# The head of a four-layer convolution kernel: GpSimd's table powers queued behind the first image's norm, TensorE's diagonals built ahead of the tables

## Chip, cores and metric

The kernel runs on one core of one Trainium2 chip. The metric is the device time of one launch in microseconds (us). Differences are told against the kernel before, and times of single events are given from the start of the profiled span.

## What is computed

The input is 32 images of 96 channels, 56 x 56. Four layers follow each other, each of the form x = x + f(norm(x)), where the norm takes groups of three channels of an image. Layer 0 is an inverted bottleneck with a gate, layer 1 a wavelet convolution, layer 2 a quantised bottleneck, layer 3 a 9 x 9 convolution with one diffusion kernel for each channel. Only the parts that the change touches are shown:

```python
# the norm ahead of each layer
g = v.reshape(B_, G, C_ // G, H_, W_)
m = jnp.mean(g, axis=(2, 3, 4), keepdims=True)
s = jnp.var(g, axis=(2, 3, 4), keepdims=True)
return ((g - m) / jnp.sqrt(s + eps)).reshape(v.shape)
...
# layer 0
h = jnp.einsum('nchw,oc->nohw', x, w_exp)
h = jax.nn.silu(_bn(h, g1, b1, m1, v1))
h = jax.lax.conv_general_dilated(h, w_dw, window_strides=(1, 1), padding='SAME', feature_group_count=MID, ...)
h = jax.nn.silu(_bn(h, g2, b2, m2, v2))
s = h.mean(axis=(2, 3))
s = jax.nn.silu(s @ w_se1.T + b_se1)
s = jax.nn.sigmoid(s @ w_se2.T + b_se2)
h = h * s[:, :, None, None]
h = jnp.einsum('nchw,oc->nohw', h, w_proj)
h = _bn(h, g3, b3, m3, v3)
return h + identity
...
# layer 3: the diffusion kernels, 9 x 9 for each channel
gauss = 1.0 / (4.0 * math.pi * tg) * jnp.exp(-r2 / (4.0 * tg))
poi = math.gamma(1.5) / math.pi ** 1.5 * tp / jnp.power(tp * tp + r2, 1.5)
return val * gauss + (1.0 - val) * poi
```

The exponential of `gauss` and the power of `poi` are both computed as elementwise powers on GpSimd.

## The kernel before

**Layer 0, image by image.** The 576 middle channels are five blocks of 128 (the last one half full). For each image ScalarE sums the pixels and their squared deviations (L287, steps `s` and `q`), TensorE adds them over the channel groups (L292, `u` and `v`), VectorE makes mean and variance (L302, L306), GpSimd raises the variance to the power -1/2 (`deviation`, L308, the tile `rstd`), VectorE makes the bias from it (`norm_bias`, L312, the tile `nb`), and ScalarE normalises (L321, the tile `xn`). TensorE expands the channels (L335), ScalarE applies silu and writes into padded tiles (L347). The depthwise 3 x 3 convolution is shared out: for blocks 0 to 2 ScalarE makes the first tap (L355, step `f`) and VectorE the other eight (L360, step `t`), one instruction of 128 x 3136 elements each; for blocks 3 and 4 TensorE multiplies with diagonal matrices (L388, steps `a` and `c`), which are built once from the weights (L262, the tile `diag`). Then come silu (L366), the gate (L412 to L436), the projection on TensorE (L447 to L449), the residual sum on VectorE (L455), and the statistics for the next norm (L87).

**The order.** `L0_ORDER` is a list of steps written out by hand. A `+` or `-` behind a step means the next or the previous image. `run_steps` goes through it once for each image, from two ahead of the first to two after the last. Under `manual_schedule` the order of PE, VectorE and ScalarE for these steps is that of the list; GpSimd and SP, and all that stands outside, are ordered by the scheduler.

**The tables.** Layers 1 and 3 need banded matrices. Their rows are made by `tables()`, called in `layer0` ahead of the steps. It opens a pool of its own (`tables`) and calls three functions. `diffusion_kernels` makes the 9 x 9 kernels: VectorE r2 (L1134 to L1141), then GpSimd two powers of 96 x 81 elements (L1145, L1146) and the sum (L1147 to L1149). `wavelet_filters` fills three tables on VectorE (L510 to L549), zeroes its rooms on GpSimd (L538, the third on VectorE), and sends each out by a DMA on SP (L550, tensor `zwav`); the third table is built in the room of the first. `diffusion_filters` copies the kernels on GpSimd (L1158, the tile `rev`), zeroes the room of the second table (L1160), fills it with 16 copies (L1167), and sends it out (L1168, tensor `zdiff`). Many small DMAs on SP then spread the rows into matrices in HBM (L559, L586).

**The late pool.** When `tables()` returns, its pool is closed, and a pool `late` (`l0l`) is opened in its room. It holds three of the five tap buffers `h2s` (numbers 2 to 4), `hab` and `hc` (outputs of TensorE's depthwise part), `wg` (gated projection weights) and the second pair of images. Whoever writes a tile of it first waits for the tables' last DMA. Two such writers stand in the head: `eye2`, a slice of `wg` (L259), from which the 18 diagonals are multiplied (L262), and the DMA that fetches images 2 and 3 (`fetch(2)`, L211).

Of the kernel before, what the change touches and what calls it, by code (L numbers as in the profile page):

```python
# [10 lines left out]
F32 = mybir.dt.float32  # L11
# [4 lines left out]
ALU = mybir.AluOpType  # L16
# [4 lines left out]
B, C, H, W = 32, 96, 56, 56  # L21
# [5 lines left out]
NT = RT * W  # L27
W2 = W // 2
NPH = 4
W4 = W // NPH  # L30
HH = H // 2
PH = HH * NPH
NP = H // (2 * RT)
# [16 lines left out]
K_GAUSS = VAL / (4.0 * math.pi * TG)  # L50
K_POI = (1.0 - VAL) * math.gamma(1.5) / math.pi**1.5 * TP
# [7 lines left out]
MANUAL = {mybir.EngineType.PE, mybir.EngineType.DVE, mybir.EngineType.Activation}  # L59
MANUAL_SP = MANUAL | {mybir.EngineType.SP}  # L60
L0_ORDER = """
# [10 lines left out]
L2_ON_DVE = {"e00", "e20", "a301", "a201"}  # L72


class Shared:


# [35 lines left out]
    tc.keep_in_program_order(nc.sync.dma_start(dram, row))  # L113


def run_steps(step, image, order):


    for n in range(-2, B + 2):
        for s in order.split():  # L120
            b = n + s.count("+") - s.count("-")
            if 0 <= b < B:
                step[s[0]](image(b), *map(int, s.rstrip("+-")[1:]))


# [51 lines left out]
def layer0(ctx, tc, S, x, w, y0, norm1, tables, aside):  # L177
# [10 lines left out]
    nc = tc.nc  # L188
    cp = ctx.enter_context(tc.tile_pool(name="l0c", bufs=1))
# [5 lines left out]
    ND = NBLK + 1  # L195
    COL = (0, 1, 2, 3, 5)
    HALF = 64
# [7 lines left out]
    pairs = [cp.tile([C, H * NPH, 2, W4], F32, tag="xt0", name="xt0")]  # L205

    def fetch(b):

        if b < B:
            pair = pairs[b // 2 % 2]  # L210
            nc.sync.dma_start(pair, x[b // 2])  # L211
            for j in range(2):
                xs[b + j] = pair, pair[:, :, j, :]
# [13 lines left out]
    for j in range(2):  # L227
        g, b_, m, v = (mid[:, 4 * j + i, :] for i in range(4))
# [3 lines left out]
        s = cp.tile([128, ND], F32, tag=f"s{j}", name=f"s{j}")  # L232
# [16 lines left out]
    mv_all = cp.tile([C, B, 2], F32, tag="mv0", name="mv0")  # L249
    h2s = [cp.tile([128, H, W], F32, tag=f"h2{i}", name=f"h2{i}") for i in range(2)]  # L250


    tables()
    late = ctx.enter_context(tc.tile_pool(name="l0l", bufs=1))
    h2s += [late.tile([128, H, W], F32, tag=f"h2{i}", name=f"h2{i}") for i in (2, 3)]
    hab = late.tile([128, NP, 2, NT], F32, tag="hab", name="hab")
    wg = late.tile([128, ND + 1, C], F32, tag="wg", name="wg")
    eye2 = wg[:, 0, :HALF]
    nc.vector.tensor_tensor(eye2, S.ident[:, :HALF], S.ident[:, HALF:], ALU.add)  # L259
    for k in (AB, CC):  # L260
        for t in range(9):
            nc.vector.tensor_scalar(diag[:, k - AB, t, :], eye2, wdw[:, COL[k], t : t + 1], None, ALU.mult)  # L262
    h2s.append(late.tile([128, H, W], F32, tag="h24", name="h24"))
    hc = late.tile([128, 2, 2, NT], F32, tag="hc", name="hc")
    pairs.append(late.tile([C, H * NPH, 2, W4], F32, tag="xt1", name="xt1"))
    fetch(2)

    ims = {}

# [12 lines left out]
    def sums(im, name, func, bias):  # L282

        im[name] = sm.tile([C, NP], F32, tag=name, name=name)
        for i in range(NP):
            junk = pool.tile([C, 2 * RT * NPH, W4], BF16, tag="junk", name="junk", bufs=1)
            nc.scalar.activation(junk, im["xt"][:, i * 2 * RT * NPH : (i + 1) * 2 * RT * NPH], func, bias=bias,  # L287
                                 accum_out=im[name][:, i : i + 1])

    def group_sum(im, name):  # L290
        ps = psm.tile([C, NP], F32, tag="sm", name="pn")
        nc.tensor.matmul(ps, S.grp, im[name], start=True, stop=True)  # L292
        im["ps" + name] = ps

    def total(im, name):
        t = sm.tile([C, 1], F32, tag=f"t{name}", name=f"t{name}")
        nc.vector.tensor_reduce(t, im["ps" + name], AX.X, ALU.add)
        return t
# [5 lines left out]
    def deviation(im):  # L304
        ve = sm.tile([C, 1], F32, tag="ve", name="ve")
        nc.vector.tensor_scalar(ve, total(im, "s2"), 1.0 / HW, EPS_GN, ALU.mult, ALU.add)  # L306
        im["rstd"] = sm.tile([C, 1], F32, tag="rstd", name="rstd")
        nc.gpsimd.tensor_tensor(im["rstd"], ve, S.mhalf[:C, :1], ALU.pow)  # L308

    def norm_bias(im):  # L310
        im["nb"] = sm.tile([C, 1], F32, tag="nb", name="nb")
# [148 lines left out]
    def store(im):  # L460
# [11 lines left out]
    step = {  # L472
        "s": lambda im: sums(im, "s1", AF.Identity, 0.0), "u": lambda im: group_sum(im, "s1"), "m": mean,
        "q": lambda im: sums(im, "s2", AF.Square, im["nm"]), "v": lambda im: group_sum(im, "s2"),
        "w": deviation, "b": norm_bias, "n": normalise, "r": residual,
        "e": expand, "f": first_tap, "t": tap, "z": end_block, "a": depthwise_ab, "c": depthwise_c,
        "g": lambda im, i: (totals, squeeze, excite, gates, gated)[i](im),
        "p": project, "d": add, "o": store,
    }
    with tc.manual_schedule(engines=MANUAL):  # L480
        run_steps(step, image, L0_ORDER)
    store_norm(tc, S, sm, psum, mv_all, norm1, S.bias1)


# [637 lines left out]
    store_norm(tc, S, sm, psum, mv_all, norm3, None)  # L1122


def diffusion_kernels(nc, cp, w):

    n = KS * KS
    dm = cp.tile([C, 4], F32, tag="dm", name="dm")
    nc.sync.dma_start(dm, w["l3_dm"])
    yy = cp.tile([C, 2, n], F32, tag="yy", name="yy")  # L1130
    nc.sync.dma_start(yy, w["grid"])
    z = cp.tile([C, 2, n], F32, tag="z", name="z")
    for i in range(2):
        nc.vector.tensor_scalar(z[:, i, :], yy[:, 0, :], dm[:, 2 * i : 2 * i + 1], None, ALU.mult)  # L1134
        nc.vector.scalar_tensor_tensor(z[:, i, :], yy[:, 1, :], dm[:, 2 * i + 1 : 2 * i + 2], z[:, i, :],
                                       ALU.mult, ALU.add)
    nc.vector.tensor_tensor(z, z, z, ALU.mult)
    r2, arg, kern = z[:, 0], z[:, 1], yy[:, 0]
    nc.vector.tensor_tensor(r2, z[:, 0], z[:, 1], ALU.add)
    nc.vector.tensor_scalar(arg, r2, K_EXP2, None, ALU.mult)  # L1140
    nc.vector.tensor_scalar(r2, r2, TP * TP, None, ALU.add)  # L1141

    nc.gpsimd.memset(yy[:, 0], 2.0)
    nc.gpsimd.memset(yy[:, 1], -1.5)
    nc.gpsimd.tensor_tensor(kern, yy[:, 0], arg, ALU.pow)  # L1145
    nc.gpsimd.tensor_tensor(r2, r2, yy[:, 1], ALU.pow)  # L1146
    nc.gpsimd.tensor_scalar(kern, kern, K_GAUSS, None, ALU.mult)  # L1147
    nc.gpsimd.tensor_scalar(r2, r2, K_POI, None, ALU.mult)
    nc.gpsimd.tensor_tensor(kern, r2, kern, ALU.add)  # L1149
    return kern  # L1150


# [82 lines left out]
def kernel_body(tc, w, x, out):  # L1235
    nc = tc.nc
    with ExitStack() as ctx:
        cp = ctx.enter_context(tc.tile_pool(name="shared", bufs=1))
        dp = ctx.enter_context(tc.tile_pool(name="scratch", bufs=1, space=DRAM))
        S = Shared()  # L1240
        S.ident = cp.tile([128, 128], F32, tag="ident", name="ident")
        S.grp = cp.tile([C, C], F32, tag="grp", name="grp")
        S.mhalf = cp.tile([128, B], F32, tag="mhalf", name="mhalf")
        nc.gpsimd.memset(S.mhalf, -0.5)
        S.bias1 = cp.tile([C, 1], F32, tag="bb", name="bb")

        def scratch(name, shape):
            return dp.tile(shape, F32, tag=name, name=name)

        y0, y1, y2 = ([scratch(f"y{i}_{g}", [GR, H * NPH, B, W4]) for g in range(C // GR)] for i in range(3))
        norm1, norm3 = (scratch(f"norm{i}", [C, 2 * B + 1]) for i in (1, 3))
        z1, z2 = (scratch(f"zwav{v}", [C, 2, NPH, LEN * NK * NPH]) for v in (1, 2))
        z3 = scratch("zwav3", [C, 2, 2, LEN * KW * 2])
        zd = scratch("zdiff", [C, 1, NPH, LEN * NK * NPH])

        t1, td = (scratch(f"t{n}", [C, (HH + 2 * HALO) * NPH, NK * PH]) for n in ("wav1", "diff"))
        t2 = scratch("twav2", [C, PH, NK * PH])
        t3 = scratch("twav3", [C, HH, KW * HH])  # L1260

        def tables():
            with tc.tile_pool(name="tables", bufs=1) as tp:
                kernels = diffusion_kernels(nc, tp, w)
                room = wavelet_filters(nc, tp, w, z1, z2, z3)
                diffusion_filters(nc, tp, kernels, zd, room)

        layer0(tc, S, x, w, y0, norm1, tables,
               [lambda c=c: wavelet_matrices(nc, z1, z2, z3, t1, t2, t3, c) for c in range(C)]
               + [lambda c=c: matrix_rows(nc, td[c], zd[c], 1) for c in range(C)])  # L1270
        with ExitStack() as ctx2:
            k2 = Layer2(ctx2, tc, S, w, y1)

            def behind(pair):
                k2.prepare(pair)
                if not k2.stages:
                    k2.begin(min(2 * pair, C - GR))

            layer1(tc, w, y0, norm1, t1, t2, t3, y1, behind)
            k2.begin(C)  # L1280
            layer2(tc, S, k2, y1, y2, norm3)
        layer3(tc, w, y2, norm3, td, out)
# [121 lines left out]
```

## Time and profile before

| what | us |
|---|---|
| median of 3 runs | 6427.65 |
| lowest and highest of them | 6418.2, 6427.76 |
| the profiled execution | 6420.77 |
| its span | 6419.0 |
| PE busy, of the span | 6013.8 |
| VectorE busy | 5173.8 |
| ScalarE busy | 4052.9 |
| GpSimd busy | 223.1 |

In the profile, PE is TensorE's matmuls, PEld its weight loads, DVE is VectorE, ACT is ScalarE, POOL is GpSimd, SP is the engine that issues the DMAs. L12 is line 12 of the kernel before. A row of the timeline has start, duration, engine, line, operation, output and input tiles (buffer numbers left out), shape and count; the bracket at its end tells how long the engine was idle before it and what ended that. A row of waits names the engine and tile that waited, who released it, and then the total in us, how often, and the longest. The granted clock is that of TensorE as a share of full speed. The mean granted clock over the whole span was 0.975.

### The profile page before, as it was taken

The page shows a single profiled execution, that of the slowest core. Times are in us where ns is not written, and L with a number is a line of the kernel's source. Part 1 is how long each engine was busy: PE and PEld are TensorE (multiplying, and loading weights), DVE is VectorE, ACT ScalarE, POOL GpSimd, SP SyncE. Part 2 cuts the span into 40 slices and gives each one's busy share as a digit, 9 for nine tenths or more (in the row PEclk, how much of TensorE's full clock was granted, in tenths as well). Part 3 has the DMA queues.
Part 4 walks back from the last instruction along what each step waited for, and adds up shares of the span by engine and source line. Part 5 has one row for each costly group of instructions (what it writes and reads, how often), then busy time and mean ns, then how long its engine had stood idle before and what let it go on. Part 6 is the DMA issues. An engine that isn't in the chain of part 4 may idle for free.

```text
span 6419.0 us, 115759 instructions
## 1 busy us (share of the span) xinstructions
PE 6013.8 (94%) x49064; PEld 3571.1 (56%) x49064; DVE 5173.8 (81%) x5533; ACT 4052.9 (63%) x5716; POOL 223.1 (3%) x157
## 2 busy tenths in 40 slices
PE   4999999999999999999969999989999999999699
PEld 2444444444444444444435666668777777777344
DVE  6999999999999999999947666667676766776587
ACT  4676666766766667667535566567676766766355
POOL 4000000000000000000000000000000000000000
PEclk8999999999999999999979999999999999999899
DMA  3022221222211222113365866558787686964988
GB/s 95 6 48 53 45 46 32 49 55 47 42 32 43 54 49 42 32 37 40 23 86 142 150 148 146 130 30 54 39 53 41 51 43 44 51 42 29 174 254 245
DMA packets 1305765, 452.95 MB, mean 71 GB/s; under 512 B 1123151, under 2 KB 1301063, under 8 KB 1303327
## 3 DMA queue, kind: packets, MB, share of 16 engines
q1 hardware_dynamic: 1305246, 445.54, 47.5%
q8 instruction: 386, 6.32, 0.5%
q14 instruction: 133, 1.08, 0.1%
HBM read 284.44 MB, written 214.08 MB: 78 GB/s over the span
## 4 chain that ended last, share of the span: by engine, by line
PE 76%; ACT 13%; DVE 5%; DMA 3%; issue 2%; POOL 1%; SPq 1%; ACTq 0%; DVEq 0%; POOLq 0%
PE psd L388 18%; PE psd L1058 11%; PE ps L335 11%; PE ps L1039 6%; PE pc L774 6%; PE pc L1210 5%; PE psj L447 5%; ACT junk L287 4%; DVE h L360 4%; PE psj L1095 3%; ACT hi L1011 2%; ACT hpad L347 2%; PE pc L758 2%; ACT a L1029 2%; PE psj L448 2%
## 5 line engine op out<-in xcount | busy, mean ns | idle before, releaser
L360 DVE SCALAR_TENSOR_TENSOR h<-hpad,l_wdw,h 128x3136 f32<-128x3136 f32 x768 | 2662.6, 3481 | 40.7 <-ACT h L355 26.8
L1058 PE MATMUL psd<-apad,diag 64*64 64x392 bf16 x20736 | 930.3, 332 | 117.1 <-issue 62.4
L335 PE MATMUL ps<-xn,l_wexp 96*128 96x392 f32 x2560 | 894.5, 501 | 32.6 <-ACT xn L321 31.5
L1058 PEld LDWEIGHTS <-diag 64*64 64x64 bf16 x20736 | 699.3, 107 | 343.7 <-issue 170.3
L388 PE MATMUL psd<-hpad,diag 64*64 64x392 f32 x9216 | 831.1, 511 | 0.0
L347 ACT ACTIVATE hpad<-ps,o,s 128x784 f32<-128x784 f32 x512 | 546.6, 1082 | 305.0 <-PE ps L335 301.8
L335 PEld LDWEIGHTS ps<-xn,l_wexp 96*128 96x128 f32 x2560 | 479.4, 191 | 401.7 <-issue 37.3
L604 ACT COPY T<-raw 32x112 f32<-32x112 f32 (+2 forms) x1440 | 462.8, 384 | 300.4 <-DMA raw<-tdiff 216.8
L1029 ACT ACTIVATE u<-ps,o,s 128x784 int16<-128x784 f32 x576 | 536.9, 1003 | 160.6 <-PE ps L1039 141.7
L1029 ACT ACTIVATE a<-psd,o,s 128x784 int16<-128x784 f32 x448 | 424.6, 1000 | 322.2 <-PE psd L1058 322.2
L447 PE MATMUL psj<-h,wg 128*96 128x392 f32 x1536 | 606.7, 531 | 15.3 <-ACT hpad L347 7.7
L388 PEld LDWEIGHTS psd<-hpad,diag 64*64 64x64 f32 x9216 | 346.9, 131 | 467.9 <-issue 433.3
L1039 PE MATMUL ps<-hi,l_w1q 96*128 96x392 f32 x1280 | 462.5, 361 | 9.3 <-ACT hi L1011 9.2
L1210 PE MATMUL pc<-x,T 128*112 128x416 f32 (+1 forms) x1152 | 415.4, 523 | 41.8 <-DMA X<-y 40.6
L774 PE MATMUL pc<-x,T 128*112 128x416 f32 (+1 forms) x1152 | 444.3, 522 | 0.0
L1039 PE MATMUL ps<-lo,l_w1q 96*128 96x392 f32 x1280 | 438.0, 342 | 0.0
L388 PE MATMUL psd<-hhalf,diag 64*64 64x392 f32 x4608 | 417.6, 510 | 0.0
L447 PEld LDWEIGHTS psj<-h,wg 128*96 128x96 f32 x1536 | 248.5, 166 | 284.4 <-issue 250.2
L347 ACT ACTIVATE hhalf<-ps,o,s 64x56 f32<-64x56 f32 (+1 forms) x192 | 163.7, 852 | 340.1 <-PE ps L335 338.3
L1210 PEld LDWEIGHTS pc<-x,T 128*112 128x112 f32 x1152 | 204.1, 178 | 252.6 <-issue 234.3
L366 ACT ACTIVATE hab<-psd,o,s 128x392 f32<-128x392 f32 x256 | 170.9, 672 | 254.3 <-PE psd L388 254.3
L388 PEld LDWEIGHTS psd<-hhalf,diag 64*64 64x64 f32 x4608 | 182.7, 132 | 222.9 <-issue 222.6
(209 smaller groups left out, 7653.1 us busy)
## 6 DMA issues: line engine op xcount, KB each, us to landing
X<-y SPq DMA_DIRECT2D x192, 392.0 KB
y<-xt SPq DMA_DIRECT2D x180, 392.0 KB
xt<-in_x_dram SPq DMA_DIRECT2D x16, 2352.0 KB
y<-y SPq DMA_DIRECT2D x96, 392.0 KB
xt<-y SPq DMA_DIRECT2D x96, 392.0 KB
out_dram<-y SPq DMA_DIRECT2D x96, 392.0 KB
twav<-zwav SPq DMA_DIRECT2D x768, 36.8 KB
raw<-twav SPq DMA_DIRECT2D x96, 168.0 KB
```

The costliest lines, as they stand in the source:

```text
L287: nc.scalar.activation(junk, im["xt"][:, i * 2 * RT * NPH : (i + 1) * 2 * RT * NPH], func, bias=bias, accum_out=im[name][:, i : i + 1])
L335: nc.tensor.matmul(ps[:, j, :NT], wexp[:, k * 128 : k * 128 + 128], im["xn"][:, j, rows, :].rearrange("c h w -> c (h w)"), start=True, sto ...
L347: nc.scalar.activation(window(im["pad"][k][p], p.stop - (p.start or 0), 0, 0, r0, n).rearrange("p r (w j) -> p j r w", j=2), ps[p, :, :NT] ...
L360: nc.vector.scalar_tensor_tensor(h2, window(im["pad"][k], 128, t // 3 - 1, t % 3 - 1, 0, H), wdw[:, k, t : t + 1], h2, ALU.mult, ALU.add,)
L388: nc.tensor.matmul(ps[c * HALF : (c + 1) * HALF, j, :NT].rearrange("p (r q m) -> p r q m", q=W4, m=2), diag[p, k - AB, t, :], phases(v[:, ...
L447: nc.tensor.matmul(out, wg[:, k, :], phases(im["h2"][k][:, rows], j), start=(k == 0), stop=False)
L604: nc.scalar.copy(to.rearrange("x t (p s) -> x t p s", p=NPH), v[:, k])
L774: nc.tensor.matmul(ps[:PH, to], st["T"][j][:, h, k, :], st["x"][:, j, h, of], start=False, stop=(n == NK - 1))
L1029: nc.scalar.activation(out, ps, AF.Identity, bias=o[:, c : c + 1], scale=s[:, c : c + 1])
L1039: nc.tensor.matmul(ps[:, j, :NT], w1[:, k * 128 : k * 128 + 128], im[part][:, r0 : r0 + RT, :].rearrange("c h w -> c (h w)"), start=(part ...
L1058: nc.tensor.matmul(ps[q, j, :NT].rearrange("p (r w) -> p r w", w=W), diag[p, k, t, :], v, start=(t == 0), stop=(t == 8))
L1210: nc.tensor.matmul(ps[:, :, to], st["T"][:, h, k, :], st["x"][:, h, :, of], start=(n == 0), stop=(n == NK - 1))
```

## The change

It has three parts.

First, the steps of image 0 up to its normalisation (`FIRST`: sums, deviations, power, bias, normalise) are traced before `tables()` is called, and `run_steps` leaves them out later. `tables` takes the instruction of image 0's power, and the seven GpSimd instructions of `diffusion_kernels` are told to be issued after it.

Second, `eye2` and the 18 diagonals are made before the tables, in a slice of `h2s[1]`, a tap buffer that lies outside of the late pool and isn't needed yet.

Third, and as a consequence, the late pool is opened after these, with `hab`, `wg` and the others unchanged in it.

```diff
+FIRST = "s u m q v w b n"
...
-def run_steps(step, image, order):
+def run_steps(step, image, order, done=""):
...
-            if 0 <= b < B:
+            if 0 <= b < B and not (b == 0 and s.rstrip("+-") in done):
                 step[s[0]](image(b), *map(int, s.rstrip("+-")[1:]))
...
-    tables()
-    late = ctx.enter_context(tc.tile_pool(name="l0l", bufs=1))
-    h2s += [late.tile([128, H, W], F32, tag=f"h2{i}", name=f"h2{i}") for i in (2, 3)]
-    hab = late.tile([128, NP, 2, NT], F32, tag="hab", name="hab")
-    wg = late.tile([128, ND + 1, C], F32, tag="wg", name="wg")
-    eye2 = wg[:, 0, :HALF]
+    eye2 = h2s[1].rearrange("p h w -> p (h w)")[:, :HALF]
     nc.vector.tensor_tensor(eye2, S.ident[:, :HALF], S.ident[:, HALF:], ALU.add)
     for k in (AB, CC):
         for t in range(9):
             nc.vector.tensor_scalar(diag[:, k - AB, t, :], eye2, wdw[:, COL[k], t : t + 1], None, ALU.mult)
-    h2s.append(late.tile([128, H, W], F32, tag="h24", name="h24"))
-    hc = late.tile([128, 2, 2, NT], F32, tag="hc", name="hc")
-    pairs.append(late.tile([C, H * NPH, 2, W4], F32, tag="xt1", name="xt1"))
-    fetch(2)
...
-        nc.gpsimd.tensor_tensor(im["rstd"], ve, S.mhalf[:C, :1], ALU.pow)
+        im["pow"] = nc.gpsimd.tensor_tensor(im["rstd"], ve, S.mhalf[:C, :1], ALU.pow)
...
     with tc.manual_schedule(engines=MANUAL):
-        run_steps(step, image, L0_ORDER)
+        for s in FIRST.split():
+            step[s](image(0))
+    tables(ims[0]["pow"].ins)
+    late = ctx.enter_context(tc.tile_pool(name="l0l", bufs=1))
+    h2s += [late.tile([128, H, W], F32, tag=f"h2{i}", name=f"h2{i}") for i in (2, 3)]
+    hab = late.tile([128, NP, 2, NT], F32, tag="hab", name="hab")
+    wg = late.tile([128, ND + 1, C], F32, tag="wg", name="wg")
+    h2s.append(late.tile([128, H, W], F32, tag="h24", name="h24"))
+    hc = late.tile([128, 2, 2, NT], F32, tag="hc", name="hc")
+    pairs.append(late.tile([C, H * NPH, 2, W4], F32, tag="xt1", name="xt1"))
+    fetch(2)
+    with tc.manual_schedule(engines=MANUAL):
+        run_steps(step, image, L0_ORDER, FIRST)
...
-def diffusion_kernels(nc, cp, w):
+def diffusion_kernels(tc, cp, w, behind):
+    nc = tc.nc
...
-    nc.gpsimd.memset(yy[:, 0], 2.0)
-    nc.gpsimd.memset(yy[:, 1], -1.5)
-    nc.gpsimd.tensor_tensor(kern, yy[:, 0], arg, ALU.pow)
-    nc.gpsimd.tensor_tensor(r2, r2, yy[:, 1], ALU.pow)
-    nc.gpsimd.tensor_scalar(kern, kern, K_GAUSS, None, ALU.mult)
-    nc.gpsimd.tensor_scalar(r2, r2, K_POI, None, ALU.mult)
-    nc.gpsimd.tensor_tensor(kern, r2, kern, ALU.add)
+    with tc.issue_after(behind):
+        nc.gpsimd.memset(yy[:, 0], 2.0)
+        nc.gpsimd.memset(yy[:, 1], -1.5)
+        nc.gpsimd.tensor_tensor(kern, yy[:, 0], arg, ALU.pow)
+        nc.gpsimd.tensor_tensor(r2, r2, yy[:, 1], ALU.pow)
+        nc.gpsimd.tensor_scalar(kern, kern, K_GAUSS, None, ALU.mult)
+        nc.gpsimd.tensor_scalar(r2, r2, K_POI, None, ALU.mult)
+        nc.gpsimd.tensor_tensor(kern, r2, kern, ALU.add)
```

In the planned order of the changed kernel, the third wavelet table's memset (L538) and its 16 copies (L549) stand behind the first and the second tap of image 0 on VectorE, where they stood ahead of the first. On SP one small DMA (L559) changes place with the third table's DMA (L550).

## Prediction

> **What bounds the kernel now.** I read the granted clock and busy time by stretch first, then the waits of the first 110 us, then the timeline of the head, and at last the chain of waits there. The table by stretch (length, then busy us of PE, PEld, DVE, ACT, POOL, then clock, DMA share and GB/s):
>
> ```profile
> 0.00:100.00 100.00, 22.41 (x58) 12.39 (x58) 47.28 (x243) 37.45 (x45) 64.79 (x59) 0.90 0.41 112
> 100.00:200.00 100.00, 86.63 (x588) 42.44 (x589) 97.49 (x64) 69.20 (x84) 5.11 (x2) 0.92 0.17 45
> 400.00:500.00 100.00, 97.82 (x624) 47.37 (x623) 93.08 (x53) 65.04 (x76) 3.63 (x1) 0.98 0.06 16
> ```
>
> From 200 us on layer 0 runs at TensorE's pace, image after image, and the page shows the same digits to slice 19. Between 100 and 200 us VectorE is the full one. Before 100 us only GpSimd is busy (65 us of 100), and the other three wait. So the head is a delay ahead of a stream that has no slack: what it loses, the end loses. The waits (engine and tile, who released it, us in total, times, longest):
>
> ```profile
> PE ps L335 <- ACT xn L321: 31.5, 1, 31.5
> ACT xn L321 <- DVE nb L312: 29.0, 1, 29.0
> DVE nb L312 <- POOL rstd L308: 20.8, 1, 20.8
> POOL zt L1160 <- DMA zwav<-zt: 19.0, 1, 19.0
> DVE wg L259 <- DMA zdiff<-zt: 7.1, 1, 7.1
> ```
>
> The first three are one wait seen from three engines: image 0's norm waits for one small GpSimd power. The timeline (start, us, engine, line) shows what stands ahead of it, and what follows:
>
> ```profile
> 22.02 13.39 POOL L1145 TENSOR_TENSOR yy<-yy,z 96x81 f32<-96x81 f32 x1 [0.78 <-DVE ws L506]
> 36.05 13.28 POOL L1146 TENSOR_TENSOR z<-z,yy 96x81 f32<-96x81 f32 x1
> 51.51 0.58 POOL L308 TENSOR_TENSOR rstd<-ve,mhalf 96x1 f32<-96x1 f32 x1
> 52.12 0.15 DVE L312 TENSOR_TENSOR nb<-nm,rstd 96x1 f32<-96x1 f32 x1 [20.84 <-POOL rstd L308]
> 60.97 2.16 DVE L538 MEMSET zt<- 96x2520 f32 x1 [0.47 <-issue]
> 63.16 1.46 DVE L549 COPY zt<-G 96x25 f32<-96x25 f32 x16
> 68.31 21.09 DVE L360 SCALAR_TENSOR_TENSOR h<-hpad,l_wdw,h 128x3136 f32<-128x3136 f32 x6 [3.69 <-ACT h L355]
> 73.80 16.75 POOL L1167 COPY zt<-rev 96x27 f32<-96x27 f32 x16
> 96.46 0.22 DVE L259 TENSOR_TENSOR wg<-ident 128x64 f32<-128x64 f32 x1 [7.06 <-DMA zdiff<-zt]
> 100.00 3.01 DVE L262 TENSOR_SCALAR diag<-wg,l_wdw 128x64 f32<-128x64 f32 x18
> ```
>
> `ve` was ready at 24.5 (L306, 24.39 plus 0.14) and its power began at 51.51. A second stall follows on VectorE: `wg` lies in the pool that is opened once the tables are done, so its first write waits for the last table's DMA; 18 multiplies for `diag` then stand among the taps. The chain of waits agrees: both powers, the copies of L1167, the DMA zdiff, then the taps to 193 us, then PE.
>
> **What the Trainium skill says.** "SBUF — State Buffer", section "SBUF: two separate sides": VectorE and GpSimd share one port pair as an exclusive lock; a VectorE operation with two SBUF inputs takes it, against a GpSimd operation that reads SBUF, and the one that started first keeps it for its whole instruction. The taps (L360) have two SBUF inputs. The trace agrees for GpSimd as the loser:
>
> ```profile
> L308 POOL TENSOR_TENSOR rstd<-ve,mhalf x4: 583/3644/3729, 51.5 to 296.0; 96x1 f32<-96x1 f32 x4
> 78.85 3.57 POOL L1167 COPY zt<-rev 96x18 f32<-96x18 f32 x2
> ```
>
> The same power took 583 ns with no tap running and 3644 beside one (a tap is 3484). Of the table's copies two get through at each tap boundary, one blocked for 3.42 us and one of 0.15; the last seven took 1.1 us together once VectorE stood still. A fill (L1160, write only) beside taps kept its pace: 2.62 us for 3024 elements, where one of 6048 with VectorE still took 5.14. For VectorE as the loser the trace disagrees: two-input operations of L515 to L519 ran in 0.17 us each while L1145's power was under way, as they did at 52 us with none. "TensorE: Matmul & The Clock Gate", part 1, says an idle TensorE starts again at half speed. Here too (clock 0.50 from 79 to 115 us), but before and after the edit it idles some 20 to 30 us at the same two places, so I count nothing.
>
> **The change, part by part.** The planned order of each engine, compared, is the same from image 1's second tap on; only the head of VectorE, GpSimd and SP differs.
>
> 1. *Image 0's power goes ahead of the two large powers.* They and their five followers and nine `rev` copies (22.0 to 51.5) now come behind it. With `ve` at 24.5 plus 0.1, 0.58 of power and 0.1, `nb` would come at 25.3 in place of 52.12.
>
> 2. *Diagonals ahead of the tables.* 18 x 0.163 (2.93 us in the chain) move to the time before image 0's sums are there (18.66 us; VectorE's first operation was at 14.91). They need `wdw`, whose landing the trace doesn't show; its DMA is issued just behind `mid`'s, which landed at 15.5. I take 16.0: the diagonals end at 19.0, two products behind them, `nm` at 19.25 for 18.85, so 0.4 later (bounds: 0, and 2 if `wdw` lands at 17.6). That gives `nb` at 25.7, 26.4 earlier. From `nb` to the first tap were 16.2 us of ScalarE and PE, unchanged: first tap at 41.9. VectorE's tables up to there (1.2 + 4.8 + 1.6 + 4.9 + 1.9 from the rows of 25.7 to 31 and 52.3 to 60.5 us) end at 40.1, beside that. Gone from between the taps: the 2.9 and the sum of 0.2.
>
> 3. *No early user of the late pool on VectorE.* `eye2` now lies in `h21`: the 7.1 us wait goes. Next on that pool is ScalarE's first tap of block 2 (`h22`), costed under 5.
>
> 4. *The third wavelet table moves between taps.* Its memset and 16 copies (2.16 + 1.46) lay before the first tap in ScalarE's shadow; in the new order they follow tap 1 and tap 2: +3.6. The memset waits for the first zwav DMA to leave the room; before, its data moved from 31.2 to 41 us, now it is issued at about 32, so done by 42, and the memset is due at 45: no wait (+2 if late).
>
> Sum on VectorE, up to image 1's `ve`: 26.4 + 7.1 + 0.2 + 2.9 - 3.6 = 33.0 us earlier: `ve` (111.78) at 78.8, its `nb` (122.28) due at 89.3.
>
> 5. *What GpSimd's queue now does beside taps.* Behind image 0's power: L1145 25.7 to 39.1, L1146 to 52.4; three followers, each at a tap boundary, to 63; nine `rev` copies, two a boundary, helped by the 1.5 us gap at 77 to 79 where VectorE waits for PE (L297), to 78; memset 2.6 to 80.5; 16 copies: six at the boundaries up to 89.3, and ten when VectorE stands, 1.7; then image 1's power 0.6. So `nb` comes at some 92 in place of 89.3: a new wait of 3 us on VectorE with the taps queued behind it, and ScalarE's normalise of image 1, which had 15 us to spare (122.3 to 137.7). Bounds: 0 if the copies pass faster, and, if the second power crawls under the taps because it fetches its operands piece by piece, most of it is left at 89.3: 9 + 1.3 + 1.7 + 2.6 + 3.4 + 0.6 = 18.6. I take 3: L1145 ran beside some forty small two-input operations and lost 0.11 us to L1146, which had none. zdiff's DMA is then issued at 91.5 and lands at 97.3 (5.8); ScalarE's first tap of block 2 (2.9) ends at 100.2, while its taps on VectorE begin three taps after `nb`, at 102.5. Image 2's fetch, behind zdiff on SP at 97 as before, lands by 115; its sums (183 before) come at 153. SP's small transfers follow and end by 170, ahead of the first store (311 before).
>
> Net at image 1: 33.0 - 3 = 30 earlier; PE joins at its wait for image 2's sums (197.76), and the rest of the order is unchanged, so the span ends 30 earlier. The profiled execution took 6420.77 (span 6419.0): 6390.8. The median shown is 6427.65, 6.9 above it, with one of three runs at 6418.2; I give the forecast against the median: 6397.6.
>
> **Rivals.** *GpSimd starves* under the taps, part 5's upper end: gain 33.0 - 18.6 = 14.4, 6413.2. For it: a blocked `rstd` power each image; against: L1145's pace. *The lock holds the other way*: tap 1 at 41.9 waits for L1146's end at 52.4, 10.5 us: gain 22.5, 6405.1. The skill's sentence speaks for it, the small operations at 24 to 26 us against. *It is swallowed*: something fixed in time holds image 2, say its fetch; 6427.65. The 38 us to spare speak against, and the planned order has the power moved, so that it does nothing is out. *Slower*: the granted clock in layer 0. An image took 97.3 us at clock 1.00 (psd from 220.86 to 318.18) and 98.9 at 0.98; if starting without the long pause made the throttle grant 0.01 less over 29 images, each is 1.5 longer, 44 in all: 6441. It decides against the change from 30 / 29 = 1.0 us an image. Nothing in the profile but the step at 300 us speaks for it.
>
> **How the numbers follow.** Forecast as told 0.73, starved 0.12, lock 0.08, swallowed 0.04, slower 0.03. A measurement here can tell about 0.2%, 12.9 us: the first three are faster (0.93), the fourth is the same, the last slower. The range reaches down to no new wait with the runs' lower level (6427.65 - 33 - 9.5, rounded up, as both at once are rare: 6386) and up to the starved end, 6413.2, so 6414.
>
> **What would show it.** Right: ScalarE's wait for `nb` falls from 29.0 to about 2; first tap near 42; no wait for zdiff on VectorE; a few us of VectorE waiting for image 1's `rstd`; layer 0's 98.9 us an image unchanged. Wrong: L1146 well over 13.3 us, a tap longer than 3.5 near 42 us, VectorE standing for zwav at 45, ScalarE waiting for zdiff with PE behind it, or a lower clock after 300 us.

## Result, and the profile after

Over five runs each the kernel after took 6393.05 us (median; 6377.03 to 6403.04) and the kernel before 6427.65: ratio 0.9949, 95% interval 0.9933 to 0.9964. That is 34.6 us less, with 23 to 43 inside the interval; 6397.6, 30 less, was forecast. The profiled executions lie further apart: span 6375.2 for 6419.0, so 43.8 less. The engines' work is the same to a few us (PE 6012.5, VectorE 5173.6, ScalarE 4051.7); only GpSimd is busier, 236.1 for 223.1.

Waits of the first 110 us of the kernel after that matter here:

```profile
ACT h L349 <- DMA zdiff<-zt: 5.7, 1, 5.7
PE ps L329 <- ACT xn L315: 4.4, 1, 4.4
DVE nb L306 <- POOL rstd L302: 2.8, 2, 2.4
ACT xn L315 <- DVE nb L306: 1.8, 1, 1.8
DVE zt L546 <- issue: 0.5, 1, 0.5
```

The three long waits for image 0's norm (31.5, 29.0, 20.8) are down to 4.4, 1.8 and 0.45 plus one new wait of 2.4; GpSimd's 19.0 for zwav and VectorE's 7.1 for zdiff are gone, and a wait of 5.7 for zdiff now stands on ScalarE. The head in the timeline of the kernel after:

```profile
15.65 3.06 DVE L260 TENSOR_SCALAR diag<-h,l_wdw 128x64 f32<-128x64 f32 x18 [0.72 <-DMA l_wdw<-in_l_wdw_dram]
24.38 0.58 POOL L302 TENSOR_TENSOR rstd<-ve,mhalf 96x1 f32<-96x1 f32 x1 [4.88 <-DVE ve L300]
24.99 0.15 DVE L306 TENSOR_TENSOR nb<-nm,rstd 96x1 f32<-96x1 f32 x1 [0.45 <-POOL rstd L302]
25.16 13.27 POOL L1155 TENSOR_TENSOR yy<-yy,z 96x81 f32<-96x81 f32 x1
38.40 13.27 POOL L1156 TENSOR_TENSOR z<-z,yy 96x81 f32<-96x81 f32 x1
41.35 3.48 DVE L354 SCALAR_TENSOR_TENSOR h<-hpad,l_wdw,h 128x3136 f32<-128x3136 f32 x1 [1.74 <-ACT h L349]
...
52.31 3.47 POOL L1158 TENSOR_SCALAR z<-z 96x81 f32<-96x81 f32 x1
59.30 17.38 POOL L1168 COPY rev<-yy 96x9 f32<-96x9 f32 x9
76.61 2.61 POOL L1170 MEMSET zt<- 96x3024 f32 x1
79.29 11.43 POOL L1177 COPY zt<-rev 96x27 f32<-96x27 f32 x16
90.69 0.57 POOL L302 TENSOR_TENSOR rstd<-ve,mhalf 96x1 f32<-96x1 f32 x1
91.29 0.16 DVE L306 TENSOR_TENSOR nb<-nm,rstd 96x1 f32<-96x1 f32 x1 [2.35 <-POOL rstd L302]
```

The rows in order of time: the diagonals are done at 18.7, image 0's power comes at 24.38 without a queue, both large powers keep 13.27 us although the first tap (L354) starts inside the second, and GpSimd's short operations then crawl through the taps (a multiply of 0.48 us beside no tap took 3.47 beside one, nine tiny copies 17.4), and image 1's power ends 2.35 us too late.

To see where the end's 43.8 us come from, two lines near a boundary are enough. The norm ahead of layer 1 and the one ahead of layer 3 each make one small power (`row`); a row of this view has durations, then the times of the first and the last. Before:

```profile
L107 POOL TENSOR_TENSOR row<-nve,mhalf x2: 5429/5433/5437, 3269.7 to 5957.5; 96x32 f32<-96x32 f32 x2
```

After:

```profile
L110 POOL TENSOR_TENSOR row<-nve,mhalf x2: 5429/5434/5439, 3239.5 to 5902.0; 96x32 f32<-96x32 f32 x2
```

At the end of layer 0 the change is worth 30.2 us (3269.7 to 3239.5), which is the forecast. At image 0's statistics (the first aggregate of L88, L91 after) it is 30.8 (218.0 to 187.2), so it is all earned in the head and carried through 32 images at 99.0 us each, as before. The other 13.6 us of the profiled pair arise behind layer 0, in code that the change doesn't touch: 25.3 less between the two `row`s (2687.8 to 2662.5), of which 11.7 are given back from the second `row` to the end (461.5 to 473.2).

### The profile page after: what moved, and what is told of

Read it like the earlier page. It is cut to its first block, busy times and chain, and to the rows that moved or that the text cites. A ratio compares the mean times of both kernels' runs of the same rounds, so it can differ in the third digit from the quotient of the medians.

```text
span 6375.2 us, 115759 instructions
## 1 busy us (share of the span) xinstructions
PE 6012.5 (94%) x49064; PEld 3561.4 (56%) x49064; DVE 5173.6 (81%) x5533; ACT 4051.7 (64%) x5716; POOL 236.1 (4%) x157
## 4 chain that ended last, share of the span: by engine, by line
PE 72%; ACT 14%; DMA 6%; DVE 4%; SPq 2%; issue 1%; POOL 1%; ACTq 0%; DVEq 0%; POOLq 0%
PE psd L382 18%; PE psd L1066 11%; PE ps L329 11%; PE pc L782 6%; PE ps L1047 6%; PE psj L441 5%; ACT junk L281 4%; PE psj L1103 3%; DVE h L354 2%; DMA raw<-tdiff 2%; ACT hi L1019 2%; DMA X<-y 2%; ACT hpad L341 2%; PE psj L442 2%; PE pc L766 2%; ACT a L1037 2%
## 5 line engine op out<-in xcount | busy, mean ns | idle before, releaser
L354 DVE SCALAR_TENSOR_TENSOR h<-hpad,l_wdw,h 128x3136 f32<-128x3136 f32 x768 | 2662.4, 3481 | 37.3 <-ACT h L349 23.5
L1047 PE MATMUL ps<-hi,l_w1q 96*128 96x392 f32 x1280 | 461.5, 361 | 9.2 <-ACT hi L1019 9.2
L341 ACT ACTIVATE hhalf<-ps,o,s 64x56 f32<-64x56 f32 (+1 forms) x192 | 163.6, 852 | 342.3 <-PE ps L329 340.5
L1220 PEld LDWEIGHTS pc<-x,T 128*112 128x112 f32 x1152 | 203.7, 178 | 264.7 <-issue 236.1
```

What stands on the lines that cost most here:

```text
L341: nc.scalar.activation(window(im["pad"][k][p], p.stop - (p.start or 0), 0, 0, r0, n).rearrange("p r (w j) -> p j r w", j=2), ps[p, :, :NT] ...
L354: nc.vector.scalar_tensor_tensor(h2, window(im["pad"][k], 128, t // 3 - 1, t % 3 - 1, 0, H), wdw[:, k, t : t + 1], h2, ALU.mult, ALU.add,)
L1047: nc.tensor.matmul(ps[:, j, :NT], w1[:, k * 128 : k * 128 + 128], im[part][:, r0 : r0 + RT, :].rearrange("c h w -> c (h w)"), start=(part ...
L1220: nc.tensor.matmul(ps[:, :, to], st["T"][:, h, k, :], st["x"][:, h, :, of], start=(n == 0), stop=(n == NK - 1))
```

## The experiments

The theory: the gain is the head's alone, and it is the sum of the prediction's parts. Rivals: the parts overlap (less than the sum, one edit nearly worthless alone); GpSimd's new backlog costs more than the 2.35 us seen; the lock against taps acts in the other direction as well; a part of the gain is made behind the head. All kernels below were measured against the kernel before on the same chip; there its median was 6398 to 6403.

**1. Powers alone.** The kernel after, with the diagonals back behind the tables, in `wg`:

```diff
-    eye2 = h2s[1].rearrange("p h w -> p (h w)")[:, :HALF]
-    nc.vector.tensor_tensor(eye2, S.ident[:, :HALF], S.ident[:, HALF:], ALU.add)
-    for k in (AB, CC):
-        for t in range(9):
-            nc.vector.tensor_scalar(diag[:, k - AB, t, :], eye2, wdw[:, COL[k], t : t + 1], None, ALU.mult)
...
     wg = late.tile([128, ND + 1, C], F32, tag="wg", name="wg")
+    eye2 = wg[:, 0, :HALF]
+    nc.vector.tensor_tensor(eye2, S.ident[:, :HALF], S.ident[:, HALF:], ALU.add)
+    for k in (AB, CC):
+        for t in range(9):
+            nc.vector.tensor_scalar(diag[:, k - AB, t, :], eye2, wdw[:, COL[k], t : t + 1], None, ALU.mult)
```

> The changed kernel with the diagonals back behind the tables, so that only the order of GpSimd's powers is changed. My theory: the two parts are not a sum. The first tap comes at 41.4 us, but after six taps VectorE stands before its first write to the late pool, at 69.5, while GpSimd still has three of the nine rev copies, the memset and 16 copies ahead of it (7.5 us alone) and the zdiff DMA (5.8): that write comes at about 83 us where it was 96.5, 13.5 us earlier, and the median is about 6414. Rival, a sum of parts: of the 30 us some 10 belong to the late pool's stall and the diagonals, so the order alone gives 20 and 6408. Rival, the norm's wait is the whole matter: 26 us and 6402.

Measured: 6387.98 for 6402.35, ratio 0.9977 [0.9968, 0.9987]. The 14.4 us by medians (8 to 20 inside the interval) fit my 13.5 as well as the rival's 20; the trace has to decide. In it image 0's statistics come at 199.2, 18.8 earlier than before, and `row` 19.0 earlier. The timeline of this kernel:

```profile
45.21 2.16 DVE L546 MEMSET zt<- 96x2520 f32 x1 [1.42 <-DMA zwav<-zt]
59.21 10.84 POOL L1168 COPY rev<-yy 96x9 f32<-96x9 f32 x9
72.66 2.52 POOL L1177 COPY zt<-rev 96x27 f32<-96x27 f32 x16
81.09 0.23 DVE L480 TENSOR_TENSOR wg<-ident 128x64 f32<-128x64 f32 x1 [11.60 <-DMA zdiff<-zt]
```

VectorE still waits for zdiff, 11.6 us for 7.1, but as it stands still from 69.5 on, GpSimd's copies go through at once (16 in 2.52 us, where 11.43 were needed beside taps), and zdiff lands sooner. Two things were missing from my 13.5: these quick copies, and that the order here puts a seventh tap ahead of the write to `wg`, where six stood. By the trace the sum-of-parts rival, 20, was right.

**2. Diagonals alone.** The kernel before, with only the diagonals moved:

```diff
+    eye2 = h2s[1].rearrange("p h w -> p (h w)")[:, :HALF]
+    nc.vector.tensor_tensor(eye2, S.ident[:, :HALF], S.ident[:, HALF:], ALU.add)
+    for k in (AB, CC):
+        for t in range(9):
+            nc.vector.tensor_scalar(diag[:, k - AB, t, :], eye2, wdw[:, COL[k], t : t + 1], None, ALU.mult)
     tables()
...
-    eye2 = wg[:, 0, :HALF]
-    nc.vector.tensor_tensor(eye2, S.ident[:, :HALF], S.ident[:, HALF:], ALU.add)
-    for k in (AB, CC):
-        for t in range(9):
-            nc.vector.tensor_scalar(diag[:, k - AB, t, :], eye2, wdw[:, COL[k], t : t + 1], None, ALU.mult)
```

> The kernel before with the diagonals built ahead of the tables in a tap buffer, and the powers where they were. My theory: the norm's wait stays (nb at 52 us), the stall of 7.1 us for zdiff goes, as do 0.2 and 3.0 us between the taps, and nothing new waits, since GpSimd gets through its copies by about 101 us, before image 1's power is asked for at 102: 10 us earlier, median about 6417. Rival: GpSimd's copies, which no longer find VectorE standing still, become late for image 1's power or for ScalarE's first tap of block 2, and half or more of the 10 us comes back as a wait: 6423.

Measured: 6391.98 for 6402.35, ratio 0.9985 [0.9977, 0.9993]; statistics at 207.7 (10.3 earlier), `row` 10.6 earlier. The norm's wait in the first 110 us:

```profile
ACT xn L320 <- DVE nb L311: 28.9, 1, 28.9
```

The norm's wait is untouched (29.0 before), and 7.1 + 2.9 + 0.2 = 10.2 are gone. The two parts give 19.0 + 10.6 = 29.6 at `row`; together they gave 30.2. They add up, by one trace each: the rival of overlap fell. The other rival, that GpSimd's copies become late, was hardly put to the test: here they ran in 2.53 us from 54.7, long before the first tap (68.1), since GpSimd's 19.0 us wait for zwav was gone as well.

**3. A room of its own for the third wavelet table.** The kernel after, with the memset back on GpSimd, and a tile that doesn't have to be vacated first:

```diff
-        if v < 2:
-            Z = rooms[v] = cp.tile([C, 2, P, LEN, P, ks], F32, tag=f"z{v}", name=f"zt{v}")
-        else:
-            n = 2 * P * LEN * P * ks
-            Z = rooms[0].rearrange("c a p e o k -> c (a p e o k)")[:, :n].rearrange(
-                "c (a p e o k) -> c a p e o k", a=2, p=P, e=LEN, o=P)
-        (nc.gpsimd if v < 2 else nc.vector).memset(Z, 0.0)
+        Z = rooms[v] = cp.tile([C, 2, P, LEN, P, ks], F32, tag=f"z{v}", name=f"zt{v}")
+        nc.gpsimd.memset(Z, 0.0)
```

> The changed kernel with a room of its own for the third wavelet table, zeroed on GpSimd while it waits for its first weights. Its 16 copies then stand before the first tap, in the time in which VectorE waits for ScalarE, and the memset leaves VectorE. My theory: the taps lie 3.6 us earlier, and since GpSimd gets fewer tap boundaries its chain ends at nearly the same time after the taps stop for image 1's nb: the wait there stays 2 to 4 us, and the net gain against the changed kernel is about 3 us, 6390. Rival: GpSimd's chain, not VectorE's, sets nb by now, nothing is gained, and the wait there grows to 6 us.

Measured: 6370.72 for 6402.35, ratio 0.9949 [0.9934, 0.9965]. The timeline:

```profile
41.41 27.99 DVE L354 SCALAR_TENSOR_TENSOR h<-hpad,l_wdw,h 128x3136 f32<-128x3136 f32 x8
87.70 0.16 DVE L306 TENSOR_TENSOR nb<-nm,rstd 96x1 f32<-96x1 f32 x1 [2.34 <-POOL rstd L302]
```

The eight taps run without a gap, `nb` comes 3.6 earlier than after (91.29), and the wait stays at 2.34: GpSimd's copies moved up with the taps. The statistics come at 183.4, 3.8 earlier than after. So step 4's 3.6 us of the prediction were a true cost, and they can be had back.

**4. No reversing copies.** Experiment 3, with the rows of the constant grid negated, so that the kernels come out in reversed order and the nine `rev` copies are not needed:

```diff
-    rev = cp.tile([C, KS, KS], F32, tag="rev", name="rev")
-    for ky in range(KS):
-        nc.gpsimd.tensor_copy(rev[:, KS - 1 - ky], kern[:, KS * ky : KS * ky + KS])
+    rev = kern.rearrange("c (y x) -> c y x", y=KS)
...
-    grid = np.stack([np.repeat(k, KS), np.tile(k, KS)])
+    grid = np.stack([np.repeat(-k, KS), np.tile(k, KS)])
```

> The same with the rows of the grid, an input table, laid out in reverse, so that the diffusion kernels come out reversed and the nine rev copies on GpSimd go. My theory: beside taps GpSimd gets two small reading operations done at each tap boundary, so that nine copies cost it 17 us; without them the table is full before 80 us, image 1's power is done (beside a tap, 3.6 us) at about 80, the wait for nb of 2.4 us and ScalarE's wait for zdiff of 5.7 us go, and with the room the net gain against the changed kernel is 6 us, 6387. Rival: the nine copies cost only their own 1.7 us, and the wait for nb stays.

Measured: 6367.96 for 6402.35, ratio 0.9945 [0.9931, 0.9959]. The timeline:

```profile
61.64 12.72 POOL L1170 COPY zt<-yy 96x27 f32<-96x27 f32 x16
74.84 3.75 POOL L302 TENSOR_TENSOR rstd<-ve,mhalf 96x1 f32<-96x1 f32 x1 [0.48 <-DVE ve L300]
85.11 0.15 DVE L306 TENSOR_TENSOR nb<-nm,rstd 96x1 f32<-96x1 f32 x1
```

Image 1's power now ends at 78.6, long before VectorE asks, and no bracket stands behind `nb`: the 2.35 us wait was the backlog's. Without the nine copies, the memset and the 16 copies for zdiff start 17.7 us sooner (58.96 for 76.61). Statistics at 181.7, 5.5 earlier than after.

**5. A pause between the powers**, to bring the second one's start into a tap. A fill of 4800 elements that nothing uses:

```diff
+        wait = cp.tile([C, 4800], F32, tag="wait", name="wait")
+        nc.gpsimd.memset(wait, 0.0)
```

> The changed kernel with a fill of 4800 elements a partition put ahead of the second power on GpSimd (about 4.1 us, write only), so that this power starts at 42.5 us, inside tap 1 (41.35 to 44.83), and not 3 us ahead of it. It settles how a long power meets the taps. My theory: a reading operation is held only until the tap that it starts in has ended, and then runs through whatever taps follow: it ends at about 58.1, with 15.6 us on its row for 13.3, the taps stay at 3.48, and image 1's nb waits some 3 us where it waited 2.35. Rival 1, each of its reads is held: over 20 us. Rival 2, the lock goes to whoever starts first, for the whole instruction: 15.6 us on its row too, and the tap behind it waits, to about 58. Rival 3, a power isn't held at all: 13.3 us.

One execution was taken, 6383.34. It tells nothing on its question: the scheduler put the fill ahead of both powers, and the second one began at 42.66, still ahead of the first tap, which the fill had moved to 43.48. One thing came by chance. The timeline shows three small copies of VectorE beside the fill:

```profile
25.35 4.09 POOL L1157 MEMSET wait<- 96x4800 f32 x1
25.51 4.00 DVE L533 COPY G<-F 96x25 f32<-96x25 f32 x3
```

The same three copies in the kernel after, beside a power:

```profile
25.42 0.33 DVE L533 COPY G<-F 96x25 f32<-96x25 f32 x3
```

**6. The pause, mended.** A third power of 24 elements, whose output nothing uses, between the two, with the order pinned by `issue_after`:

```diff
+        p1 = nc.gpsimd.tensor_tensor(kern, yy[:, 0], arg, ALU.pow)
+        with tc.issue_after(p1.ins):
+            p2 = nc.gpsimd.tensor_tensor(junk, r2[:, :24], yy[:, 1, :24], ALU.pow)
+        with tc.issue_after(p2.ins):
+            p3 = nc.gpsimd.tensor_tensor(r2, r2, yy[:, 1], ALU.pow)
```

> The changed kernel with a third power, of 24 elements and not used by anyone (0.4 + 24 x 0.16, about 4.2 us), between the two large ones, so that the second large one starts at about 42.6 us, inside tap 1 (41.35 to 44.83). In the run before this one the extra fill went ahead of both powers and held VectorE's copies for 4 us, so the power began ahead of the tap again; a power held no copy there. My theory: a reading operation is held only until the tap that it starts in has ended, and then runs through: about 15.4 us on its row, taps at 3.48. Rival 1, each of its reads is held: over 20 us. Rival 2, the lock goes to whoever has it for the whole instruction: tap 2 comes only when this power has ended, at about 58. Rival 3, a large power isn't held at all: 13.3 us.

One execution was taken, 6362.81. The timeline:

```profile
41.00 3.48 DVE L354 SCALAR_TENSOR_TENSOR h<-hpad,l_wdw,h 128x3136 f32<-128x3136 f32 x1 [1.47 <-ACT h L349]
42.67 14.94 POOL L1160 TENSOR_TENSOR z<-z,yy 96x81 f32<-96x81 f32 x1
47.03 3.36 DVE L354 SCALAR_TENSOR_TENSOR h<-hpad,l_wdw,h 128x3136 f32<-128x3136 f32 x1
```

The power takes 14.94 for 13.27, 1.7 longer; tap 1 ends at 44.48, 1.8 after the power's start. That is what a power held to the end of the tap under which it started would show: it then runs through the taps at its own pace, and no tap is longer than 3.48. Between tap 1 and tap 2 lay 2.5 us without a tap here (the third table's memset); a start with the next tap following at once wasn't tried. Starving (over 20) and taps waiting for the power (the second to 58) both fell.

The same trace says what the 2.35 us wait depends on. The third power and the 1.7 us put the start of the nine `rev` copies 6.7 us later (65.99 for 59.30), and still they end at 76.8 for 76.7, because VectorE waits for PE at that point, from 76.3 on, and lets the rest through; `nb` waits 2.35 us as before. So this much more work ahead of that gap was free, and the wait is made of what stands behind it: the memset and the 16 copies.

**7. Before and after again**, on two other chips (2 and 3 in the table), for the part that lies behind the head. No edit.

> The changed kernel once more, unchanged, beside the kernel before. The head's gain by image 0's statistics was 30.8 us in the first trace, and the whole span's 43.8. My theory: the head repeats within half a us; what differs behind layer 0 between the two traces is scatter of layers 1 to 3, so that from the first norm row to the second norm row this trace lies anywhere between 2660 and 2690 us, and the median is about 31 us below the kernel before. Rival: the changed kernel is faster there too, for a reason of its own, and the trace shows 2662 again with a median 40 or more below.

> The kernel before once more, for a second trace. By scatter its time from the first norm row to the second lies between 2660 and 2690 us and needn't be 2688 again. By the rival it is near 2688. Image 0's statistics end at 218.0 within half a us.

> The kernel before, compared with itself. If a program that is loaded once keeps an offset of its own in layers 1 to 3, the ratio to the other copy can lie outside of its interval around 1, by up to the 15 to 25 us by which the stretch from the first norm row to the second differs between traces; if each execution draws anew, it is 1 within 0.15%.

> The changed kernel again, beside two copies of the kernel before. Head alone: 30 to 31 us below, ratio 0.9952. An advantage behind the head too, as the last comparison of 48 us would have it: 0.9926 again. An offset kept by each loaded program: anywhere from 15 to 50 us below, and different from both earlier comparisons.

The change measured 0.9926 [0.9913, 0.994] on the first of these chips and 0.9956 [0.9941, 0.9971] on the second; the kernel before against a second copy of itself 1.0 [0.9991, 1.001], which shows no offset between one copy of a program and another. The traces (us; "rows" is the time between the two `row`s; the last column is PE's waits in layer 2 that nothing in the profile explains):

| trace | image 0's statistics | first `row` | rows | span | PE, issue |
|---|---|---|---|---|---|
| before | 218.0 | 3269.7 | 2687.8 | 6419.0 | 62.4 |
| before, chip 2 | 218.2 | 3270.0 | 2669.5 | 6396.2 | 52.2 |
| before, chip 3 | 220.3 | 3273.4 | 2671.5 | 6401.7 | 50.0 |
| after | 187.2 | 3239.5 | 2662.5 | 6375.2 | 41.3 |
| after, chip 2 | 186.4 | 3241.0 | 2682.7 | 6383.9 | 58.2 |
| after, chip 3 | 186.3 | 3239.7 | 2656.3 | 6352.4 | 40.1 |

Up to the first `row` the change is worth 30.2, 29.0 and 33.7. Of the last, some 2 us go with the clock in that trace of the kernel before, whose statistics come at 220.3 (experiment 8). Behind it each kernel scatters by 18 to 26 us, in both directions: on chip 2 the kernel after is the slower one there. The waits of layer 2 (900 us behind the first `row` to the second one) go with it. Before, in the first profile:

```profile
PE psd L1058 <- issue: 62.4, 39, 6.2
```

After:

```profile
PE psd L1066 <- issue: 41.3, 42, 3.6
```

And after, on chip 2:

```profile
PE psd L1066 <- issue: 58.2, 43, 3.9
```

The same code waits 41.3 us in one execution and 58.2 in another, so the first pair's 21 us between before and after is not shown to be an effect of the change. What these waits are the profile doesn't show. TensorE's mean granted clock over that stretch goes with them in part: 0.99 in the first and the third trace after, 0.98 in the other four.

The 48 us by medians of chip 2 stay open. Its traces show 29.0 at the end of layer 0 and the opposite sign behind it, but the profiled run after is the slowest of the six there (6385.76; the others 6349.51 to 6369.38). The clock is a rival that these runs don't rule out: those five had a mean granted clock of 0.977 or 0.978, the slowest 0.975, and the eleven runs before 0.975 or 0.976. Among the kernel before's own runs on the chip of experiments 1 to 4, the eleven at 0.977 took 10.7 us less on average than the eight at 0.975 (6397.1 and 6407.8). Whether the change has a share in the clock isn't shown; on chip 3 both kernels ran between 0.974 and 0.978.

**8. Experiment 4 again**, beside the kernel after on chip 3.

> The version with the room of its own and without the rev copies, beside the changed kernel on one chip. By the heads it is 4.5 to 5.5 us below it (image 0's statistics at 181.7 for 187.2, less 1.6 for a throttle step that comes an image earlier), so some 35 below the kernel before; with offsets of 15 us from one load to the next, the medians can't show it, and the head of its trace must: statistics at 181.7 within half a us.

Measured: 6368.18, ratio 0.995 [0.9935, 0.9965], beside 6372.45 for the kernel after. `nb` comes at 85.50, again without a wait, but the statistics at 185.1, only 1.2 earlier than the kernel after on that chip, where I had expected 5. Two waits of VectorE in image 1's later taps show where it went: the one for ScalarE's first tap (L349) was 2.35 for 0.92 in experiment 4, and the one for PE's projection (`psj`) 3.65 for 2.04. In this trace:

```profile
DVE xt L449 <- PE psj L443: 3.7, 1, 3.7
```

In experiment 4:

```profile
DVE xt L449 <- PE psj L443: 2.0, 1, 2.0
```

The difference goes with TensorE's granted clock. It stood at 0.50 from 139.9 to 146.7 us here and from 163.6 to 167.2 again, which is worth 5.1 us at full speed; in experiment 4 it did so from 140 to 143.4 only, worth 1.7. The 3.4 us between them are what the statistics came later (185.1 for 181.7). The kernel before does the same: in its trace on chip 3, with two such stretches ahead of 203 us, also worth 5.1, the two waits are 2.4 and 3.7 and the statistics come at 220.3; in its other two traces, with none there, the first wait is absent, the second 2.0, and the statistics come at 218.0 and 218.2. So the delay is one of the execution and not of this version. In experiment 4 the head of this version was the earliest of all that ran, and it is faster than the kernel before by 0.5% twice, but the 4.3 us between the two medians lie within the scatter of either: that it beats the kernel after is not shown.

## Why the prediction was right

The forecast, 6397.6, is 4.6 us above the median, and its mechanism holds at each step, narrowly at step 4. That the steps came out within a us is more than the median can say, whose interval is 20 us wide; it is the trace's head that bears them out:

- **Step 1** (`nb` at 25.3): 24.99, with the power at 24.38. It comes 27.1 us sooner, where 26.4 were counted with step 2's delay.
- **Step 2** (diagonals, 0.4 late; first tap at 41.9): `wdw` landed at 15.6 for the assumed 16.0, and the diagonals were done at 18.7, at about the moment when the sums came. The 0.4 fell away, and the first tap came at 41.35. Alone, this part and step 3 gave 10.6 for the 10.2 that the rows say.
- **Step 3** (no wait for zdiff on VectorE): gone. ScalarE waits for it instead, 5.7 us, and its first tap of block 2 ends at 99.67 (100.2 was worked out), before VectorE needs it. So this wait costs nothing.
- **Step 4** (+3.6, the zwav room free in time): the memset and the copies took 2.16 + 1.45 between taps, and there was only 0.47 of idle time ahead of them. Experiment 3 got 3.8 back. But the cover was thin: in the two repeats of the kernel after the same memset did wait for zwav, 0.73 and 1.30, and 1.42 in experiment 1. The room came free at 44.6 to 45.2 there, not by 42 as the prediction had it; that this cost nothing in the first trace was a matter of less than 1 us, and so luck.
- **Sum**: image 1's `ve` at 78.36, forecast 78.8.
- **Step 5** (`nb` at 92, wait 3): 91.29, wait 2.35. On the way the powers ended at 51.7, the followers at 59.2 (63 forecast: only two of the three were held to a tap's end), `rev` at 76.7, the copies at 90.7. Experiment 4 takes the nine copies away, and the wait goes. The prediction's picture of it, some copies passing between taps and the rest when VectorE stands, fits experiment 6, where more work ahead of the gap at 77 left the wait as it was.
- **Net** 30: 30.8 at image 0's statistics, 30.2 at the end of layer 0.

What the prediction argued less well is why the second power doesn't starve. It took L1145's pace beside some forty small operations as the reason. Experiment 6 gives a fuller one: the power is held once, if it starts under a tap (1.7 us), and not at all if it is already running, as in the kernel after. Had the second power started just inside a tap, it would by this one execution have lost about that tap, 3.5 us, and not come near the bound of 18.6. The rival with the lock the other way falls too: taps of 3.48 and 3.36 us ran beside a power that had started first. Here the Trainium skill ("SBUF — State Buffer", section "SBUF: two separate sides") says that whoever starts first keeps the lock for its whole instruction; the measurement shows that for the tap, and not for the power.

The rival of a lower clock didn't come true: an image still took 99.0 us. What the prediction called the step at 300 us, from 97.3 to 98.9 us an image, is no lasting lower clock either. In the first trace after, TensorE stood at 0.50 from 363.0 to 366.3 us and at 1.00 around it, behind a pause of 1.75 us in which TensorE waited for ScalarE's sums. The average of 10 us is then 0.83 (columns as in the prediction's table by stretch):

```profile
360.00:370.00 10.00, 8.40 (x22) 4.00 (x23) 6.42 (x8) 1.51 (x4) 3.63 (x1) 0.83 0.16 46
```

Such an image is 1.6 us longer (image 0 to image 1 took 98.94 in experiment 3, where the stretch came at 261, and 97.35 after). Which image has it first isn't set by the head's length: behind image 0's statistics it came at 393 us in two traces of the kernel before and at 277 in the third, and at 363, 341 and 264 in those of the kernel after, whose heads are alike within a us. Experiment 3's gain of 3.8 at the first image, 2.7 at the end of layer 0, has lost 1.6 to it at image 1.

The 4.6 us between forecast and median need no cause of their own: the same kernel's runs spread over 26 us.

## What to carry to other kernels

When a stream behind the head has no slack, cost a change of the head at one late marker (here the statistics of image 0), then read the same marker at the end of the layer; what differs behind it in untouched code has to be compared with repeated executions, and with the granted clock of each, before it is credited to the change. Where a slow engine's queue holds both a short operation that others wait for and long table work, put the short one first, and count how the long work's many short followers fare beside the engine that is then busy; here 25 copies held GpSimd for 28.8 us, the two powers for 26.5. Look also for the gap in which that engine stands still: what gets done up to it is free. Before moving work off a wait, look at who stands next in line for the same buffer, and whether that one has the time to wait.

## What the runs showed of the hardware that was not expected

- A GpSimd power of 96 x 81 elements that is under way runs through VectorE's two-input taps without loss on either side (13.27 us, taps 3.48 and 3.36). One that started inside a tap lost about the rest of that tap (14.94 us; one execution).
- GpSimd's fills behave differently from its reading operations: one of 3024 elements kept 2.62 us beside taps (the kernel before), but one of 4800 held three small VectorE copies for 4.00 us that take 0.33 beside a power. This is from one execution, and wasn't tried by itself.
- GpSimd's copies are cheap only when VectorE stands still: 16 of 27 elements in 2.52 us then, 11.43 to 16.75 when taps run beside them.
- Under otherwise equal work TensorE's granted clock drops to 0.50 for stretches of 3.4 or 6.8 us, in some executions and not in others. Two such stretches late in the head (5.1 us lost) came with image 0's statistics 2.2 us later in the kernel before and 3.4 later in experiment 4's.
- TensorE's waits in layer 2 without a visible cause differ by some 20 us between executions of the same code, and the distance of the two norm rows with them. This is more than half of the whole change's worth.
